# A state-space scan kernel: units of 4 states by 32 channels by 1024 tokens, scanned in place in PSUM

## Chip, cores and metric

The kernel runs on one core of one Trainium2 chip. The metric is the device time of one execution in microseconds (us). Engines are called as in the profile: PE is TensorE (PEld its weight loads), DVE VectorE, ACT ScalarE, POOL GpSimd, SP SyncE, which issues the transfers here. L388 is line 388 of the kernel whose profile is shown. SBUF and PSUM are the two on-chip memories in which the kernel's tiles lie; its matmuls write PSUM tiles.

## The reference, cut to what matters

Three Mambas (selective state spaces) carry the cost. Per Mamba there are 4 images of 4096 tokens, 384 inner channels (`d`) and 16 states (`n`):

```python
xc, z = split(x @ in_w.T)                 # 384 + 384
xc = silu(causal depthwise conv(xc) + conv_b)
dt, B, C = split(xc @ x_w.T)              # 12, 16, 16
dt = softplus(dt @ dt_w.T + dt_b)
def step(h, inp):                         # one token; h is [b, 384, 16]
    dA = exp(dt_t[..., None] * A)
    h = dA * h + (dt_t * x_t)[..., None] * B_t[:, None, :]
    return h, einsum('bdn,bn->bd', h, C_t)
y = (ys + D * xc) * silu(z)
out = y @ out_w.T
```

Stage one runs two Mambas on the same normed input and adds both. Stage two runs a third one with a layer norm before it and a depthwise 3x3 convolution, a second norm and an MLP after it. Stage three (a dynamic convolution and window mixing) is left alone by the change.

## The kernel before

512 tokens of one Mamba are called a stretch: 64 in stage one, 32 in stage two. Channels lie on the partitions, tokens along the free axis. For each of 16 states and 3 chunks of 128 channels there is one chain over a 128x512 piece, and one call of `background.step()`, which traces a piece of the work of the next stretch (projections, convolution, norms) between the scans:

```python
for n in range(n0, n0 + NG):
    for d in range(ND):
        dA = self.psum_a.tile([128, T], F32, name="dA")
        nc.scalar.activation(dA, dt[:, d, :], AF.Exp, scale=self.A[:, d, n : n + 1])
        dBx = self.work.tile([128, T], F32, name="dBx", bufs=2)
        nc.vector.tensor_tensor(dBx, dtx[:, d, :], Bs[:, n - n0, :], ALU.mult)
        h = self.work.tile([128, T], F32, name="h", bufs=3)
        st = self.state[:, d, n : n + 1]
        nc.vector.tensor_tensor_scan(h, dA, dBx, st, ALU.mult, ALU.add)
        nc.vector.tensor_copy(st, h[:, T - 1 : T])
        g = self.work.tile([128, T], F32, name="g", bufs=3)
        nc.gpsimd.tensor_tensor(g, h, Cs[:, n - n0, :], ALU.mult)
        nc.tensor.matmul(ys[d], self.ident, g, start=(n == 0), stop=(n == NS - 1))
        background.step()
# ... softplus: Abs, Exp, Ln on ScalarE, three GpSimd and one VectorE operation
```

The instructions are put into each engine's queue at build time by a scheduler that goes by its own estimate of readiness. On the chip each queue runs in the order so built.

Of the kernel before, what the change touches and what calls it, by code (L numbers as in the profile page):

```python
# [13 lines left out]
F32 = mybir.dt.float32  # L14
AF = mybir.ActivationFunctionType
ALU = mybir.AluOpType
# [4 lines left out]
NB = 4            # batch  # L21
C = 192           # channels
CP = 96           # channels per partition chunk; channel = chunk * 96 + partition
HW = 64           # image side
L = HW * HW       # tokens of one image
DI = 384          # inner width of a mamba
ND = DI // 128    # its chunks of 128
NS = 16           # states
RK = 12           # rank of dt
HID = 768         # hidden width of an MLP  # L30
NH = HID // 128
T = 512           # tokens handled at a time
NT = L // T
NG = 2            # states whose B and C are loaded together
EPS = 1e-5
WIN = 4           # window side
NPOS = WIN * WIN  # positions in a window
NWIN = L // NPOS  # windows of one image


class Pack:
    """Small arrays side by side in one [partitions, columns] array: one load, many views."""
# [27 lines left out]
def chunked(a, p):  # L70
    """[k * p + i, ...] -> [i, k, ...]"""
    a = a.reshape((a.shape[0] // p, p) + a.shape[1:])
    return np.moveaxis(a, 0, 1)


def sedenion_signs():
    """sign[i][k] of e_i * e_(i^k) in the sedenions, whose product is that sign times e_k."""
# [21 lines left out]
class Background:  # L99
    """Work of other stages, traced piece by piece between the steps of the scan in front."""  # L100
# [20 lines left out]
class Norm:  # L121
    """Layer norm of [96, 2, T] over the channels, which lie on the partitions."""
# [52 lines left out]
class Mlp:  # L175
    """gelu(x w1 + b1) w2 + b2 of [96, 2, T]; `last(k, psum)` takes the product before b2."""
# [30 lines left out]
class Mamba:  # L207
    """One selective state space, T tokens at a time: d on the partitions, time along the free
    axis. What it hands from one stretch of tokens to the next stays on chip."""

    def __init__(self, nc, name, taps, ins, const, work, psum, psum_y, psum_a, dram, ident):
        self.nc, self.name, self.taps = nc, name, taps
        self.work, self.psum, self.psum_y, self.psum_a = work, psum, psum_y, psum_a
        self.dram, self.ident = dram, ident
# [8 lines left out]
        self.conv_b, self.dt_b, self.D = w["conv_b"], w["dt_b"], w["D"]  # L223
        self.x_w, self.out_w = w["x_w"], w["out_w"]
        self.A = const.tile([128, ND, NS], F32, name=f"{name}_A")
        nc.scalar.activation(self.A, w["A_log"], AF.Exp)
        nc.vector.tensor_scalar_mul(self.A, self.A, -1.0)
        self.conv = const.tile([128, ND, taps, 128], F32, name=f"{name}_conv")
        for d in range(ND):
            for j in range(taps):  # L230
                nc.vector.tensor_scalar_mul(
                    self.conv[:, d, j, :], ident, w["conv_w"][:, d, j : j + 1]
                )
        self.halo = const.tile([128, ND, taps - 1], F32, name=f"{name}_halo")
        self.state = const.tile([128, ND, NS], F32, name=f"{name}_state")

    def front(self, xn, first, u):
        """All that the scan of these tokens needs; into the dict `u`."""
        nc, K = self.nc, self.taps
        raw = self.work.tile([128, ND, K - 1 + T], F32, name="raw", bufs=1)  # L240
        if first:
            nc.gpsimd.memset(self.halo, 0.0)
        nc.gpsimd.tensor_copy(raw[:, :, 0 : K - 1], self.halo)
        z = u["z"] = self.work.tile([128, ND, T], F32, name="z", bufs=2)
        for e in range(2 * ND):
            ps = self.psum.tile([128, T], F32, name="ps_in", tag="mm")
            for k in range(2):
                nc.tensor.matmul(  # L248
                    ps, self.in_w[:, k, bass.ts(e, 128)], xn[:, k, :], start=(k == 0), stop=(k == 1)
                )  # L250
            nc.scalar.copy(raw[:, e, K - 1 :] if e < ND else z[:, e - ND, :], ps)  # L251
            yield
        nc.gpsimd.tensor_copy(self.halo, raw[:, :, T:])
        xc = u["xc"] = self.work.tile([128, ND, T], F32, name="xc", bufs=2)
        for d in range(ND):
            ps = self.psum.tile([128, T], F32, name="ps_conv", tag="mm")
            for j in range(K):
                nc.tensor.matmul(  # L258
                    ps, self.conv[:, d, j, :], raw[:, d, j : j + T], start=(j == 0), stop=(j == K - 1)
                )  # L260
            nc.scalar.activation(xc[:, d, :], ps, AF.Identity, bias=self.conv_b[:, d : d + 1])
            yield
        nc.scalar.activation(xc, xc, AF.Silu)
        nc.scalar.activation(z, z, AF.Silu)
        yield
# [3 lines left out]
        dbl = self.work.tile([RK + 2 * NS, T], F32, name="dbl", bufs=2)  # L269
        nc.scalar.copy(dbl, ps)  # L270
        bc = u["bc"] = self.dram.tile([2 * NS, T], F32, name="bc", bufs=3)
        nc.sync.dma_start(bc, dbl[RK:, :])
        yield
        dt = u["dt"] = self.work.tile([128, ND, T], F32, name="dt", bufs=2)
        for d in range(ND):
            ps = self.psum.tile([128, T], F32, name="ps_dt", tag="mm")
            nc.tensor.matmul(ps, self.dt_w[:, bass.ts(d, 128)], dbl[:RK, :], start=True, stop=True)  # L277
            nc.scalar.activation(dt[:, d, :], ps, AF.Identity, bias=self.dt_b[:, d : d + 1])
        yield
        # softplus(s) = max(s, 0) + log1p(e), e = exp(-|s|); what 1 + e rounds off is added back  # L280
        e = self.work.tile([128, ND, T], F32, name="sp_e", bufs=1)
        nc.scalar.activation(e, dt, AF.Abs)
        nc.scalar.activation(e, e, AF.Exp, scale=-1.0)  # L283
        dtx = u["dtx"] = self.work.tile([128, ND, T], F32, name="dtx", bufs=2)
        nc.gpsimd.tensor_scalar(dtx, e, 1.0, 1.0, ALU.add, ALU.subtract)  # L285
        nc.gpsimd.tensor_tensor(dtx, e, dtx, ALU.subtract)
        nc.scalar.activation(e, e, AF.Ln, bias=1.0)
        yield
        nc.vector.scalar_tensor_tensor(dt, dt, 0.0, e, ALU.max, ALU.add)
        nc.gpsimd.tensor_tensor(dt, dt, dtx, ALU.add)  # L290
        nc.gpsimd.tensor_tensor(dtx, dt, xc, ALU.mult)  # L291
        yield

    def scan(self, u, first, background):
        nc = self.nc
        if first:
            nc.vector.memset(self.state, 0.0)
        dt, dtx, bc = u["dt"], u["dtx"], u["bc"]
        ys = [self.psum_y.tile([128, T], F32, name=f"y{d}") for d in range(ND)]
        for n0 in range(0, NS, NG):  # L300
            Bs = self.work.tile([128, NG, T], F32, name="Bs", bufs=2)
            Cs = self.work.tile([128, NG, T], F32, name="Cs", bufs=2)
            for t, r in ((Bs, n0), (Cs, NS + n0)):
                nc.sync.dma_start(t, bc[r : r + NG, :].unsqueeze(0).broadcast_to([128, NG, T]))
            for n in range(n0, n0 + NG):
                for d in range(ND):
                    dA = self.psum_a.tile([128, T], F32, name="dA")
                    nc.scalar.activation(dA, dt[:, d, :], AF.Exp, scale=self.A[:, d, n : n + 1])  # L308
                    dBx = self.work.tile([128, T], F32, name="dBx", bufs=2)
                    nc.vector.tensor_tensor(dBx, dtx[:, d, :], Bs[:, n - n0, :], ALU.mult)  # L310
                    h = self.work.tile([128, T], F32, name="h", bufs=3)
                    st = self.state[:, d, n : n + 1]
# [575 lines left out]
```

## Time and profile before

The time is 17661 us (median of 4 runs, 17657 to 17670). Profile lines are in the prediction below; the stages read:

| stage | length, us | DVE busy | PE busy | ACT busy | POOL busy |
|---|---|---|---|---|---|
| one (64 stretches) | 8705 | 8204 | 6358 | 3635 | 5976 |
| two (32 stretches) | 5540 | 3787 | 4470 | 2479 | 2964 |
| three | 3404 | 641 | 2996 | 564 | 2 |

### The profile page before, as it was taken

The numbers are of one execution on the slowest core, as the hardware profiler recorded it, in microseconds if no ns is written. First come the engines' busy times: TensorE is split into PE (matmuls) and PEld (weight loads), VectorE is DVE, ScalarE is ACT, GpSimd is POOL, SyncE is SP. The second block draws the span as 40 slices with busy tenths as digits, with TensorE's granted clock in tenths as the row PEclk, the third lists the DMA queues.
The fourth block names the chain that finished last, engine by engine and source line by source line (L and its number), as shares of the span: only waits on it lengthen the run. The fifth ranks groups of instructions, "written<-read, shape, count | busy, mean of one in ns | idle before, by whom it ended". The sixth has DMA issues, their size and how long they took to land. (4 is left out here: it accounts for less than half of the span.)

```text
span 17649.1 us, 110111 instructions
## 1 busy us (share of the span) xinstructions
PE 13823.4 (78%) x33296; PEld 6083.8 (34%) x33296; DVE 12632.4 (72%) x16123; ACT 6678.3 (38%) x8486; POOL 8941.9 (51%) x5458
## 2 busy tenths in 40 slices
PE   7777777777777777777778878888888869797989
PEld 2222222222222222222223333333333336565656
DVE  8999999999999999999787667676676720202020
ACT  4444444444444444444344444444444411111111
POOL 6766766676667667666565555555555500000000
PEclk8888888878878887888788888888888879898989
DMA  1111111111111111111111111111111110000000
GB/s 66 66 66 66 65 67 67 65 65 67 66 66 66 65 68 66 66 66 64 60 60 56 56 52 58 55 53 55 56 54 54 52 25 6 9 6 11 4 4 6
DMA packets 328063, 902.55 MB, mean 51 GB/s; under 512 B 78196, under 2 KB 111256, under 8 KB 327368
## 3 DMA queue, kind: packets, MB, share of 16 engines
q1 hardware_dynamic: 326704, 892.35, 15.1%
q8 instruction: 261, 4.28, 0.1%
q10 hardware_dynamic: 760, 3.16, 0.1%
q14 instruction: 338, 2.77, 0.0%
HBM read 851.35 MB, written 44.04 MB: 51 GB/s over the span
## 5 line engine op out<-in xcount | busy, mean ns | idle before, releaser
L316 POOL TENSOR_TENSOR g<-h,Cs 128x512 f32<-128x512 f32 x4608 | 6766.6, 1486 | 4030.0 <-PE y L317 2158.8
L317 PE MATMUL y<-g,ident 128*128 128x512 f32 x9216 | 5914.9, 758 | 2370.4 <-POOL g L316 2346.1
L313 DVE TENSOR_TENSOR_SCAN h<-dA,m_state,dBx 128x512 f32<-128x512 f32 x4608 | 5728.5, 1267 | 1121.8 <-POOL g L316 787.9
L310 DVE TENSOR_TENSOR dBx<-dtx,Bs 128x512 f32<-128x512 f32 x4608 | 5734.1, 1252 | 61.8 <-POOL dtx L291 61.8
L308 ACT ACTIVATE dA<-dt,m_A 128x512 f32<-128x512 f32 x4608 | 3158.3, 690 | 6314.1 <-DVE h L313 5977.1
L317 PEld LDWEIGHTS y<-g,ident 128*128 128x128 f32 x9216 | 1859.1, 229 | 5863.7 <-POOL g L316 4824.1
L686 DVE TENSOR_TENSOR y<-plus,neg 96x512 f32<-96x512 f32 x64 | 43.9, 686 | 1599.8 <-ACT neg L685 1599.8
L258 PE MATMUL ps_conv<-raw,m_conv 128*128 128x512 f32 x2112 | 984.5, 604 | 86.8 <-ACT z L251 61.2
L675 PE MATMUL plus<-xn,t 96*96 96x256 f32 x4352 | 1014.6, 380 | 0.0
L675 PE MATMUL minus<-xn,t 96*96 96x256 f32 x3840 | 941.4, 398 | 10.8 <-ACT xn L169 10.8
L248 PE MATMUL ps_in<-xT,m_in_w 96*128 96x512 f32 x1536 | 858.4, 673 | 113.9 <-ACT raw L251 108.6
L613 POOL MEMSET img<- 96x132 f32 x4 | 0.8, 204 | 1795.2 <-DVE xw L660 1795.2
L675 PEld LDWEIGHTS plus<-xn,t 96*96 96x96 f32 x4352 | 710.8, 163 | 339.6 <-issue 134.5
L187 PE MATMUL ps_h<-xn,t 96*128 96x512 f32 x1536 | 764.1, 637 | 76.2 <-ACT hid L190 50.2
L675 PEld LDWEIGHTS minus<-xn,t 96*96 96x96 f32 x3840 | 649.3, 171 | 253.6 <-ACT xn L169 26.7
L196 PE MATMUL ps_o<-hid,t 128*96 128x512 f32 x1536 | 681.6, 601 | 29.1 <-ACT hid L192 29.1
L277 PE MATMUL ps_dt<-dbl,m_dt_w 12*128 12x512 f32 x576 | 459.6, 922 | 243.1 <-ACT dbl L270 233.9
L314 DVE COPY m_state<-h 128x1 f32<-128x1 f32 x4608 | 630.2, 137 | 23.6
L258 PEld LDWEIGHTS ps_conv<-raw,m_conv 128*128 128x128 f32 x2112 | 399.3, 192 | 636.2 <-issue 476.3
L285 POOL TENSOR_SCALAR dtx<-sp_e 128x1536 f32<-128x1536 f32 x96 | 540.7, 5632 | 70.9 <-ACT sp_e L283 70.9
L147 PE MATMUL var<-mean_w,ln_sq 96*128 96x1 f32 x2048 | 315.9, 284 | 327.6 <-ACT ln_sq L142 327.6
L525 PE MATMUL ps_dw<-img,dw 96*96 96x512 f32 x1152 | 538.3, 617 | 0.0
(122 smaller groups left out, 11143.7 us busy)
## 6 DMA issues: line engine op xcount, KB each, us to landing
Bs<-bc SPq DMA_DIRECT2D x768, 512.0 KB, 3.6
Cs<-bc SPq DMA_DIRECT2D x768, 512.0 KB, 3.6
x<-x SPq DMA_DIRECT2D x64, 384.0 KB, 3.3
xt<-in_x SPq DMA_DIRECT2D x32, 384.0 KB, 3.4
x<-o SPq DMA_DIRECT2D x32, 384.0 KB, 2.7
img<-x SPq DMA_DIRECT2D x8, 1536.0 KB, 21.2
out<-o SPq DMA_DIRECT2D x32, 384.0 KB, 3.9
bc<-dbl SPq DMA_DIRECT2D x96, 64.0 KB, 1.6
```

What stands on the lines that cost most here:

```text
L187: nc.tensor.matmul(ps, self.w1[:, k, bass.ts(m, 128)], x[:, k, :], start=(k == 0), stop=(k == 1))
L196: nc.tensor.matmul(ps, self.w2[:, m, bass.ts(k, CP)], h[:, m, :], start=(m == 0), stop=(m == NH - 1),)
L248: nc.tensor.matmul(ps, self.in_w[:, k, bass.ts(e, 128)], xn[:, k, :], start=(k == 0), stop=(k == 1))
L258: nc.tensor.matmul(ps, self.conv[:, d, j, :], raw[:, d, j : j + T], start=(j == 0), stop=(j == K - 1))
L285: nc.gpsimd.tensor_scalar(dtx, e, 1.0, 1.0, ALU.add, ALU.subtract)
L308: nc.scalar.activation(dA, dt[:, d, :], AF.Exp, scale=self.A[:, d, n : n + 1])
L310: nc.vector.tensor_tensor(dBx, dtx[:, d, :], Bs[:, n - n0, :], ALU.mult)
L313: nc.vector.tensor_tensor_scan(h, dA, dBx, st, ALU.mult, ALU.add)
L314: nc.vector.tensor_copy(st, h[:, T - 1 : T])
L316: nc.gpsimd.tensor_tensor(g, h, Cs[:, n - n0, :], ALU.mult)
L317: nc.tensor.matmul(ys[d], self.ident, g, start=(n == 0), stop=(n == NS - 1))
L675: nc.tensor.matmul(ps[:, m, :], w["sed"][:, cc, s ^ k, bass.ts(m, CP)], xn[:, cc, bass.ts(s, NWIN)], start=(n == 0 and cc == 0), stop=(n = ...
```

## The change

Its intent: take the `dt*x*B` multiply off VectorE, where it contended with GpSimd, and the state copy too. To let one instruction multiply by B or C for a whole tile, a unit is now 4 states x 32 channels on the 128 partitions by 1024 columns (one Mamba's 1024 tokens in stage one; two groups of channels by 512 tokens in stage two). `dt`, `dt*x`, B and C are stored to DRAM and read back, repeated over the partitions. The scan overwrites the `Exp` result in PSUM. Three of four C multiplies go to VectorE, the fourth stays on GpSimd. The sum over states becomes a matmul with 32 output columns, four of them in the four column groups. Softplus is one function of ScalarE. 24 units make a stretch, 2304 the whole program. Cut to its core:

```diff
-        nc.scalar.activation(dA, dt[:, d, :], AF.Exp, scale=self.A[:, d, n : n + 1])
-        nc.vector.tensor_tensor(dBx, dtx[:, d, :], Bs[:, n - n0, :], ALU.mult)
-        nc.vector.tensor_tensor_scan(h, dA, dBx, st, ALU.mult, ALU.add)
-        nc.vector.tensor_copy(st, h[:, T - 1 : T])
-        nc.gpsimd.tensor_tensor(g, h, Cs[:, n - n0, :], ALU.mult)
-        nc.tensor.matmul(ys[d], self.ident, g, start=(n == 0), stop=(n == NS - 1))
+    def inputs(self, u):                         # w: S + 3 buffers, 7 in stage one, 5 in two
+        self.nc.gpsimd.tensor_tensor(w, blk["used"]["dtx", c, s], b, ALU.mult)
+    def decay(self, u):                          # a: PSUM, 2 buffers of 2 banks
+        self.nc.scalar.activation(a[:, p, :], ..., AF.Exp, scale=blk["m"].A[:, q, j : j + 1])
+    def run(self, u, on_pool):
+        h = w if on_pool else a
+        nc.vector.tensor_tensor_scan(h[:, p, :], a[:, p, :], w[:, p, :], ..., ALU.mult, ALU.add)
+        nc.scalar.copy(state, h[:, :, self.ts - 1])
+        (nc.gpsimd if on_pool else nc.vector).tensor_tensor(w, h, cc, ALU.mult)
+    def add_up(self, u):                         # once per four units (two in stage two)
+        nc.tensor.matmul(y[32 * g : 32 * g + 32, f : f + T], self.sel, ws[s][:, p, f : f + T], ...)
+    # stream(), at step i:
+            self.load(unit(i + self.AHEAD)); self.inputs(unit(i + 2)); self.decay(unit(i + 1))
+            self.run(unit(i), i % 4 == 1)
+            step(units[i][0])                    # background work, as before
+            self.add_up(unit(i - 1))             # when unit i - 1 ends its group
+            self.gate(unit(i - 3))
+    # evacuations of matmul results: the next matmul is traced first, then a yield
-            nc.scalar.activation(dt[:, d, :], ps, AF.Identity, bias=self.dt_b[:, d : d + 1])
-        ... Abs, Exp, Ln, and four more operations
+            nc.scalar.activation(dt[:, d, :], ps, AF.Softplus, bias=self.dt_b[:, d : d + 1])
```

## The prediction

> **What bounds the kernel now.** I read the page first, then the windows view cut where the work changes, then the groups by form, then single lines. The program is three stages in a row: two Mambas over 512 tokens at a time (64 stretches), a third Mamba with depthwise conv and MLP (32 stretches), and a last stage that the change leaves alone. I cut at the last output store of stage one (8706 us) and the first image load of stage three (14244 us). Columns: length, then busy us (and instructions) of PE, PEld, DVE, ACT, POOL, then clock, DMA share, GB/s.
> ```profile
> 0.00:8705.00 8705.00, 6357.87 (x11773) 2369.33 (x11774) 8203.83 (x10050) 3635.42 (x4761) 5975.76 (x3598) 0.81 0.19 66
> 8705.00:14245.00 5540.00, 4470.03 (x9669) 1766.10 (x9667) 3787.32 (x5097) 2478.89 (x3072) 2963.76 (x1851) 0.85 0.16 54
> 14245.00:17649.00 3404.00, 2995.52 (x11856) 1948.39 (x11856) 641.23 (x976) 563.99 (x653) 2.43 (x10) 0.90 0.05 9
> ```
> Stage one is bound by VectorE: 8204 of 8705 us, 94%, so 136 us per stretch. Stage two is bound by no single engine (PE 81%, DVE 68%) at 173 us per stretch; it waits in chains. Stage three is PE at 88%.
>
> What fills VectorE, from the groups by form:
> ```profile
> L316 POOL TENSOR_TENSOR g<-h,Cs 128x512 f32<-128x512 f32 x4608 | 6766.6, 1486 | 4030.0 <-PE y L317 2158.8 <-DVE h L313 1595.1 <-issue 133.6
> L317 PE MATMUL y<-g,ident 128*128 128x512 f32 x9216 | 5914.9, 758 | 2370.4 <-POOL g L316 2346.1
> L310 DVE TENSOR_TENSOR dBx<-dtx,Bs 128x512 f32<-128x512 f32 x4608 | 5734.1, 1252 | 61.8 <-POOL dtx L291 61.8
> L313 DVE TENSOR_TENSOR_SCAN h<-dA,m_state,dBx 128x512 f32<-128x512 f32 x4608 | 5728.5, 1267 | 1121.8 <-POOL g L316 787.9 <-ACT xc L263 329.2 <-issue 0.6
> L308 ACT ACTIVATE dA<-dt,m_A 128x512 f32<-128x512 f32 x4608 | 3158.3, 690 | 6314.1 <-DVE h L313 5977.1 <-POOL dt L290 235.1 <-DVE m_state L314 90.8
> ```
> A multiply (L310) costs as much as a scan, with equal element counts. The one-line views (min/median/max) show that this is not its own work:
> ```profile
> L310 DVE TENSOR_TENSOR dBx<-dtx,Bs x4608: 656/816/3921, 86.5 to 14091.4; 128x512 f32<-128x512 f32 x192
> L313 DVE TENSOR_TENSOR_SCAN h<-dA,m_state,dBx x4608: 1245/1271/1285, 87.7 to 14094.2; 128x512 f32<-128x512 f32 x192
> L316 POOL TENSOR_TENSOR g<-h,Cs x4608: 1251/1271/2883, 89.0 to 14095.6; 128x512 f32<-128x512 f32 x192
> ```
> The scan never varies; the multiply and its POOL partner do. Alone, L310 takes 0.66 us, so of its 5734 us some 2700 us are spent blocked.
>
> **What the Trainium skill says.** (1) "SBUF — State Buffer", Who interferes with whom: a VectorE instruction with two SBUF inputs contends with a GpSimd instruction that reads SBUF, one with a single SBUF input does not. The trace agrees: L310 (two SBUF inputs) is 0.66 to 3.9 us, L313 (one PSUM, one SBUF) stays within 1.245 to 1.285. (2) "GPSIMD Engine Reference", 3.1: 4497 ns for a 2048-element fp32 tensor_tensor. The trace has 1251 ns at 512 and 3414 at 1536 (L286), 2.11 ns an element, which extends to 4496. (3) "TensorE: Matmul & The Clock Gate", Part 3: matmuls with 32 output columns in distinct column groups run concurrently (2.38 times for three); no 32-column matmul is in this trace.
>
> **The change part by part.** A unit is 4 states x 32 channels x 1024 columns, twice a 128x512 piece: 2304 units in place of 4608 pieces; 24 units per stretch.
>
> *VectorE.* Removed: 4608 dBx multiplies (5734 us, now on POOL), 4608 state copies of 137 ns (630 us, now on ACT). Kept: all scan elements. Added: three quarters of the h*C multiplies (1728 of 1024), a quarter stays on POOL. Scan cost: additions from PSUM take 680 ns at 512 (L508) and 1216 at 1024 (L140), so 1.05 ns per element; L323, which like the scan has a scalar per partition and a PSUM input, takes 737 at 512, so about 200 ns are fixed. If the scan's fixed part is the same, 1271 is 200 plus 2.09 ns per element, and 1024 as one instruction cost 2.34 us, 2.29 back to back (two L313 in a row show 2.44 us, so 50 ns overlap). In stage two it stays two of 512: 2.44. The C multiply reads h from PSUM: L140 is the same form (PSUM and SBUF, 1024 columns), 1.216 us, 1.17 overlapped. Both now have one SBUF input, so POOL should not block them. Four units, stage one: 4x2.29 + 3x1.17 = 12.7 us; stage two: 4x2.44 + 3x1.17 = 13.3 us. Per stretch (six fours): 76 and 80 us. Beside that, stage one has 1.5 gates of 1.22 and 2.5 us of norm and output (L364, L365, L371, L413): floor 80 us. Stage two has two norms (4x1.21), gates, image and MLP additions (7x0.7): floor 90 us.
>
> *POOL.* 1.25 multiplies of 1024 per unit at 178 + 1024x2.11 = 2.34 us: 70 us per stretch, plus 4 for dt*x and 2 for the norm: 76. The Softplus function removes L285, L286, L290 (5.6+3.4+3.7 us) and, with the gate moved to VectorE, L326 (3.9).
>
> *ACT.* Exp at 1024: 692 + 512x0.836 (slope from L142 and L263) = 1.12 us; 24 of them 27 us; state copies 24x0.25 (about L366's fixed cost) = 6; projections, Silu, Softplus 11. Table loads of 1283 ns: the instruction order of the built kernel has 584 in stage one and 480 in stage two (before 439 and 377), so 12 and 19 us per stretch. Total 57 and, with MLP and norms, 85 us.
>
> *PE.* Eight back-to-back instructions of 512 columns took 3.70 us (L258), (3.70-0.59)/7 = 0.44 each, two per fp32 matmul: 0.89 us. The 48 sums per stretch remain 48 matmuls. One behind the other: 43 us, as before. Each matmul is two passes on one column group, so I expect the second pass of one group to run beside the first of the next: half, 21 us. The rest of stage two is 81 matmuls of 512 columns plus small ones, 77 us, plus 3 for D: 101 us halved, 123 if nothing overlaps. Stage one: 56 or 78, no bound.
>
> *DMA.* Each unit brings 0.5 MB (dt, dtx, B, C shares), plus stores: about 33 MB per 1024 tokens of one Mamba, near 185 GB/s at the new pace. Before, 892 MB took 15.1% of the span, so the engines move about 335 GB/s when busy. It fits.
>
> *The wait I expect instead.* dA has two PSUM buffers, and the scan now overwrites it, so a buffer comes free only after the C multiply. In the built order, 227 of 384 fours of stage one place the multiply of unit 0 after the scan of unit 1; then Exp of unit 2 starts only when VectorE has nothing else left: 1.12 + handoff, 1.3 us. That is 0.59x1.3x6 = 4.6 us per stretch. ACT's table switches between two Exps (load, Silu, load: 4 us) I put at 5 us, waits at block starts for the trip through DRAM at 2. Stage one: 80+4.6+5+2 = 92 us, x64 = 5.89 ms. Stage two: PE 101, VectorE 90, ACT 85 in order and coupled; I choose 118 us, x32 = 3.78 ms. Stage three 3.40, start 0.09. Sum 13.16 ms.
>
> **The rivals.** *PE becomes stage two's bound* (no overlap of column groups): 123 us is a floor, about 135 with waits, 4.3 ms, total 13.7. For it: every fp32 matmul in the trace is two instructions (L317 has 9216 for 4608), and both passes of one sum use the same group. *ACT stalls VectorE in both stages*: more loads and only two dA buffers; if each of some 4.5 switches per stretch costs a full 3 us, stage one goes to 100 us, total 13.7. *DMA latency binds*: one SP queue carries stores and loads in order, and loads of a block follow its stores. Against it: loads run six units (20 us) ahead and land in 3.6 us. It would add 5 to 10 us a stretch, 13.8. *PSUM in-place scan is slower*: 10% more per scan is 5.5 us a stretch, 0.5 ms. *All hides well*: 86 and 102 us, 12.25 ms.
>
> **Range and chances.** The low end is the last rival, 12.3; the high end takes two of the bad ones together, 14.3. Even both stages 25% over my figures give 15.6 ms, still 12% faster, so the direction is nearly safe; what is left is an unforeseen serial trip through DRAM.
>
> **What would show it.** L310's successor on POOL near 2.34 us and the C multiply on VectorE near 1.22 with min and median together: contention gone. Scan at 2.34 us: in place in PSUM costs nothing. VectorE 85 to 90% busy in stage one, its idle time ended by the Exp on ACT. PE's sums in stage two: busy time halved or not. Stage lengths 5.9, 3.8, 3.4 ms. I am wrong if the scan is much slower in PSUM, if POOL's multiply is well above 2.4 us, or if VectorE waits on POOL or DMA for most of its idle time.

## More of the kernel before

In stage one the length minus VectorE's busy time is only 501 us: VectorE is the bound. In stage two no engine fills the time.

## The result

The time after is 14731 us (median of 4 runs, 14730 to 14734) against 17661. The ratio is 0.834, with a 95% interval of 0.8328 to 0.8351. A ratio is the mean time of one kernel's fast runs over that of the other's of the same rounds, so not quite the ratio of the medians quoted. The result is correct. So the direction was right, but the time is 1571 us over the prediction and 431 us over the upper end of its range.

The windows view of the kernel after, cut at the same three places (columns as in the prediction):

```profile
0.00:6830.00 6830.00, 4624.21 (x12160) 1449.60 (x12160) 5185.57 (x3365) 3334.64 (x4707) 4819.34 (x2312) 0.78 0.49 167
6830.00:11323.00 4493.00, 3705.09 (x9856) 1384.17 (x9856) 2842.03 (x2563) 2546.56 (x3854) 2433.56 (x1200) 0.82 0.41 130
11323.00:14728.00 3405.00, 2993.60 (x11856) 1946.24 (x11856) 641.37 (x978) 563.93 (x653) 3.35 (x14) 0.90 0.05 9
```

Stage three is untouched (3405 against 3404). Stage one is 6830 us where I had 5.98 ms with the start; stage two 4493 where I had 3.78. VectorE's busy time is what I said: 5186 us in stage one, 81 per stretch (predicted 80), 2842 in stage two, 89 per stretch (predicted 90). So nothing is wrong with the work. What is wrong is the time in which VectorE stands: 6830 - 5186 = 1644 us in stage one (predicted 12 per stretch, 0.77 ms, and 0.09 of start) and 4493 - 2842 = 1651 us in stage two (predicted 118 - 90 = 28 per stretch, 0.90 ms). **The miss is VectorE's idle time, about 0.78 ms more in stage one and 0.75 in stage two.**

The groups by form of the kernel after, for the parts that the prediction timed (busy us, mean ns, then idle time of the engine ahead of them and who ended it):

```profile
L398 DVE TENSOR_TENSOR w<-dA,u_C 128x1024 f32<-128x1024 f32 x1728 | 2060.1, 1210 | 456.2 <-ACT m_state L396 455.7 <-PE ps_y L420 0.5
L388 DVE TENSOR_TENSOR_SCAN dA<-dA,m_state,w 128x1024 f32<-128x1024 f32 x864 | 2006.8, 2346 | 634.0 <-ACT m_state L396 416.3 <-POOL w L369 145.0 <-ACT dA L376 52.4
...
L398 POOL TENSOR_TENSOR w<-w,u_C 128x1024 f32<-128x1024 f32 x576 | 1352.0, 2347 | 622.6 <-ACT m_state L396 622.6
...
L420 PE MATMUL ps_y<-w,sel 128*32 128x512 f32 x9216 | 2616.8, 757 | 1954.1 <-POOL w L398 1303.9 <-DVE w L398 647.3
```

The scan takes 2346 ns (predicted 2.34 us), the C multiply 1210 (1.216), GpSimd's multiply 2347 (2.34), and the 9216 passes of the sums 2617 us in place of 5915 (predicted half). Two idle terms stand out. Ahead of the sums TensorE stood 1954 us, and two thirds of that was ended by GpSimd's C multiply, which does only a quarter of them. And VectorE's waits are ended chiefly by ScalarE's state copy, an instruction of 158 ns. (A wait is put down to what came last: in the timeline below the `Exp` that the scan needs ended only 0.08 us before the copy.)

### How one hold goes round the engines

The timeline of the kernel after, in stage one (start us, duration, engine, instruction; in brackets the engine's idle time ahead of it and who ended it):

```profile
2652.04 9.26 POOL L369 TENSOR_TENSOR w<-u_dtx,u_B 128x1024 f32<-128x1024 f32 x4 [9.58 <-PE ps_y L420]
...
2657.07 4.60 DVE L388 TENSOR_TENSOR_SCAN dA<-dA,m_state,w 128x1024 f32<-128x1024 f32 x2 [4.07 <-ACT m_state L396]
2658.04 0.57 ACT L296 COPY dbl<-ps_x 44x512 f32<-44x512 f32 x1
...
2659.64 1.28 ACT L309 ACT_TABLE_LOAD   x1
2661.26 2.35 POOL L398 TENSOR_TENSOR w<-w,u_C 128x1024 f32<-128x1024 f32 x1
...
2663.66 1.92 PE L420 MATMUL ps_y<-w,sel 128*32 128x512 f32 x2 [6.30 <-POOL w L398]
...
2665.51 3.78 PE L303 MATMUL ps_dt<-dbl,m_dt_w 12*128 12x512 f32 x4
...
2667.62 0.69 ACT L309 ACTIVATE dt<-ps_dt,m_pack 128x512 f32<-128x512 f32 x1 [6.69 <-PE ps_dt L303]
2668.32 1.28 ACT L376 ACT_TABLE_LOAD   x1
...
2669.62 1.12 ACT L376 ACTIVATE dA<-u_dt,m_A 128x1024 f32<-128x1024 f32 x1
2670.67 0.15 ACT L396 COPY m_state<-dA 128x1 f32<-128x1 f32 x1
2670.84 2.36 DVE L388 TENSOR_TENSOR_SCAN dA<-dA,m_state,w 128x1024 f32<-128x1024 f32 x1 [8.05 <-ACT m_state L396]
```

Read it from the top. GpSimd, released by the end of a group of sums, does four B multiplies in a row, and only then, at 2661.26, the C multiply. TensorE's queue has the sums that take that product at its head, so it stands 6.30 us. Behind them wait the matmuls of `ps_dt`, whose input (`dbl`) was ready at 2658.6. They then take 3.78 us for four passes, where the same four take 1.98 at another place of this trace (3003.34): TensorE comes out of the wait at half its rate. ScalarE has the evacuation of `ps_dt` (the instruction that reads the matmul's result out of PSUM) at the head of its queue and stands 6.69 us, with a load of its function table before and one after it. The `Exp` and the state copy, which need nothing of all this, come behind it. VectorE stands 8.05 us. The same sequence, a TensorE wait of 6.3 us ended by GpSimd and a VectorE wait of about 8.0 ended by ScalarE, returns all through stage one: 20 times between 975 and 6526 us.

The Trainium skill states the rule behind it ("PSUM — Partial Sum Buffer", Engine vs sequencer instructions): the queues of ScalarE, VectorE and GpSimd are strict first-in-first-out, and matmuls start and complete in program order. This trace agrees, with 6.30, 6.69 and 8.05 us. On the rate the skill ("TensorE: Matmul & The Clock Gate", Part 1) says that the clock gate passes every pulse or half of them, as the array is found busy or idle; 3.78 against 1.98 us fits.

The waits view, between 600 and 6200 us of the kernel after, for TensorE, ScalarE and VectorE (who waited for whom: us in total, times, longest):

```profile
PE ps_y L420 <- POOL w L398: 878.8, 218, 11.1
PE ps_y L420 <- DVE w L398: 508.9, 172, 11.4
```

```profile
ACT xc L284 <- PE ps_conv L275: 357.4, 74, 10.1
...
ACT dt L309 <- PE ps_dt L303: 175.2, 35, 6.7
```

```profile
DVE dA L388 <- ACT m_state L396: 459.9, 141, 8.1
DVE w L398 <- ACT m_state L396: 216.2, 66, 7.6
...
DVE m_y L433 <- PE ps_y L420: 118.5, 19, 14.0
```

### The profile page after: what moved, and what is told of

Read it like the earlier page. It is cut to its first block, busy times and chain, and to the rows that moved or that the text cites. A ratio compares the mean times of both kernels' runs of the same rounds, so it can differ in the third digit from the quotient of the medians.

```text
span 14728.2 us, 102888 instructions
## 1 busy us (share of the span) xinstructions
PE 11322.9 (77%) x33872; PEld 4780.0 (32%) x33872; DVE 8669.0 (59%) x6906; ACT 6445.1 (44%) x9214; POOL 7256.2 (49%) x3526
## 5 line engine op out<-in xcount | busy, mean ns | idle before, releaser
L369 POOL TENSOR_TENSOR w<-u_dtx,u_B 128x1024 f32<-128x1024 f32 x2304 | 5351.1, 2350 | 2499.2 <-PE ps_y L420 2157.9
L420 PE MATMUL ps_y<-w,sel 128*32 128x512 f32 x9216 | 2616.8, 757 | 1954.1 <-POOL w L398 1303.9
L388 DVE TENSOR_TENSOR_SCAN dA<-dA,m_state,w 128x512 f32<-128x512 f32 (+1 forms) x1872 | 3281.8, 1772 | 970.3 <-ACT m_state L396 570.5
L376 ACT ACTIVATE dA<-u_dt,m_A 128x1024 f32<-128x1024 f32 (+1 forms) x3072 | 2758.3, 902 | 1040.3 <-DVE w L398 818.7
L398 DVE TENSOR_TENSOR w<-dA,u_C 128x1024 f32<-128x1024 f32 x1728 | 2060.1, 1210 | 456.2 <-ACT m_state L396 455.7
L398 POOL TENSOR_TENSOR w<-w,u_C 128x1024 f32<-128x1024 f32 x576 | 1352.0, 2347 | 622.6 <-ACT m_state L396 622.6
L420 PEld LDWEIGHTS ps_y<-w,sel 128*32 128x32 f32 x9216 | 412.9, 121 | 3757.4 <-POOL w L398 1677.0
L388 DVE TENSOR_TENSOR_SCAN w<-dA,m_state,w 128x512 f32<-128x512 f32 (+1 forms) x624 | 1087.1, 1759 | 254.3 <-POOL w L369 156.3
L388 DVE TENSOR_TENSOR_SCAN dA<-dA,w 128x1024 f32<-128x1024 f32 (+1 forms) x432 | 824.7, 1931 | 409.1 <-POOL w L369 160.0
L841 PE MATMUL minus<-xn,t 96*96 96x256 f32 x3840 | 939.2, 397 | 11.8 <-ACT xn L171 11.7
L376 ACT ACT_TABLE_LOAD x527 | 676.1, 1283 | 9.4
L407 PE MATMUL ps_y<-u_xc,m_D 128*128 128x512 f32 x576 | 393.7, 803 | 350.8 <-DVE m_y L433 345.0
```

The lines of the kernel that those rows point to most:

```text
L369: self.nc.gpsimd.tensor_tensor(w, blk["used"]["dtx", c, s], b, ALU.mult)
L376: self.nc.scalar.activation(a[:, p, :], blk["used"]["dt", c, s][:, p, :], AF.Exp, scale=blk["m"].A[:, q, j : j + 1])
L388: nc.vector.tensor_tensor_scan(h[:, p, :], a[:, p, :], w[:, p, :], 0.0 if blk["first"] else state[:, p : p + 1], ALU.mult, ALU.add,)
L398: (nc.gpsimd if on_pool else nc.vector).tensor_tensor(w, h, cc, ALU.mult)
L407: nc.tensor.matmul(y[:, f : f + T], blk["m"].D[:, c, :], blk["used"]["xc", c][:, f : f + T], start=True, stop=False, skip_group_check=True,)
L420: nc.tensor.matmul(y[32 * g : 32 * g + 32, f : f + T], self.sel, ws[s][:, p, f : f + T], start=False, stop=q == NQ - 1, skip_group_check=True,
```

## The experiments

Fifteen kernels ran, all timed in three rounds against the kernel before. "Idle" is the stage's length minus VectorE's busy time, from the windows view. Stage three stayed near 3405 us in all and is left out.

| run | what is different from the kernel after | time, us | ratio to before | stage one: length, idle | stage two: length, idle |
|---|---|---|---|---|---|
| (after) | - | 14731 | 0.834 | 6830, 1644 | 4493, 1651 |
| state_dve | state copy on VectorE | 14555 | 0.8244 | 6599, 1349 | 4544, 1511 |
| no_switch | no table switches (wrong) | 14163 | 0.8022 | 6507, 1365 | 4248, 1404 |
| light_pe | one tap per convolution (wrong) | 14442 | 0.8178 | 6942, 1753 | 4100, 1270 |
| w_more | 9 and 6 `w` buffers | 14531 | 0.8229 | 6770, 1637 | 4368, 1536 |
| four_gone | the four above together (wrong) | 13508 | 0.7649 | 6274, 974 | 3819, 832 |
| grouped | Silu and Softplus in one piece each | 14660 | 0.8302 | 6754, 1556 | 4481, 1631 |
| conv_twice | Mamba convolutions done twice | 15426 | 0.8735 | 7239, 2071 | 4779, 1930 |
| no_pool_c | all C multiplies on VectorE | 14334 | 0.8118 | 6510, 985 | 4411, 1337 |
| pool_first | GpSimd's C multiply on unit 0 of 4 | 14437 | 0.8175 | 6510, 1408 | 4531, 1686 |
| npc_conv_twice | no_pool_c + conv_twice | 14739 | 0.8345 | 6703, 1155 | 4623, 1544 |
| npc_light_pe | no_pool_c + light_pe (wrong) | 14194 | 0.8039 | 6408, 891 | 4360, 1299 |
| npc_grouped | no_pool_c + grouped | 14192 | 0.8035 | 6435, 906 | 4346, 1271 |
| npc_grouped_sd1 | that + state copy of stage one on VectorE | 14095 | 0.7982 | 6342, 714 | 4336, 1261 |
| npcgs_pin | that + norm operations of stage two pinned later | 14090 | 0.7981 | 6335, 708 | 4349, 1269 |
| h_sbuf | h written to SBUF, not over dA | 15196 | 0.8608 | 7158, 1002 | 4636, 1406 |

The letters of theories in the quoted expectations were given anew in each batch, and each text says what they stand for.

### First batch: four suspects, one at a time

The waits named the state copy, the table loads, TensorE's late results and the `w` buffers. Each was taken away alone.

**state_dve**: the copy leaves ScalarE's queue.

```diff
-        nc.scalar.copy(state, h[:, :, self.ts - 1])
+        nc.vector.tensor_copy(state, h[:, :, self.ts - 1])
```

> One edit: the state copy goes from ACT to VectorE. Theory A (VectorE is held by ACT's queue in order: evacuations that wait for TensorE and table switches stand ahead of Exp and of the state copy): the copy leaves that queue, but Exp stays in it, and VectorE gets 2304 copies of 0.14 us, 0.32 ms, so only part of the 1.26 ms of waits for the copy comes back: 14.2 to 14.6 ms. Rival D (the copy itself on the path, between scan and C multiply on another engine, is the cause): all of the 1.26 ms less 0.32 comes back, 13.8 ms. Rival B (too few w buffers, POOL and TensorE wait for each other): 14.7 to 15.0 ms.

Measured 14555 us (14547 to 14567): 176 us less, as theory A had it. Stage one gains 231, stage two loses 51. The loss has a visible part: 192 copies of two columns from SBUF average 781 ns, one of them taking 5.1 us, while the 576 of the same shape from PSUM average 152. The trace of the kernel after shows what the copy's place costs: each of the 1728 C multiplies on VectorE starts 0.03 to 8.3 us after its unit's copy on ScalarE has ended, and none before, though it does not read what the copy writes.

**no_switch**: Silu, Sqrt and Gelu become Identity and Softplus becomes Exp, so that one table serves.

> Wrong result on purpose: Silu, Softplus, Sqrt and Gelu of the two scan stages replaced by Identity and Exp, so that no table is switched there (1064 loads of 1.283 us gone from ACT, all else in place). Theory A: VectorE's waits for ACT hold 193 us of table loads directly and as much again in what the loads delay: 14.1 to 14.4 ms. Rival E (table switches are the main thing that my prediction mis-sized): 13.5 ms. Rivals B and C (w buffers, TensorE load): 14.6 to 14.7.

Measured 14163 us: 568 us less, in theory A's range, for 1141 table loads of 1283 ns (1.46 ms of ScalarE), all but three taken away, 0.50 us a load. (72 of them were in stage three, whose length did not change; for the others it is 0.53.) It is the largest of the four, but about a third of the miss.

**light_pe**: one matmul per convolution (of 4, 3 and 9).

```diff
-            for j in range(K):
+            for j in (K - 1,):                      # start and stop both True
```

> Wrong result on purpose: one tap of each convolution is kept (4 or 3 taps to 1, 9 to 1), which takes 9 matmuls of 0.89 us from each stretch of stage one and 22 from each of stage two: 0.51 and 0.63 ms of TensorE work, none of any other engine. Theory A and C (background results come late from TensorE and are waited for in order by ACT and VectorE): 13.8 to 14.2 ms, and ACT's idle time behind ps_conv falls. If TensorE is only busy and not in the way (B, D, E): 14.6 ms or more.

Measured 14442 us, between the two expectations: 289 us less. Stage two gained 393 us and stage one lost 112 though TensorE did less. Its granted clock there fell from 0.78 to 0.74:

```profile
0.00:6942.00 6942.00, 4281.30 (x11008) 1276.60 (x11008) 5188.92 (x3365) 3344.18 (x4719) 4815.67 (x2312) 0.74 0.48 164
```

ScalarE's waits behind `ps_conv` did fall, as expected (357 to 103 us between 600 and 6200 us). Taking this work away did not shorten stage one. I took that for the clock at this point; see conv_twice and npc_light_pe.

**w_more**: two more `w` buffers in stage one, one more in stage two. There is no room for them, so the second Mamba shares the first one's convolution weights. That is wrong in principle, though its output stayed within the tolerance.

> Wrong result on purpose (stage one's second Mamba uses the first one's conv taps, which frees the memory): 9 in place of 7 buffers for w in stage one, 6 in place of 5 in stage two. Rival B (POOL waits 2.16 ms for TensorE to give w back, TensorE waits for POOL's product, and VectorE waits 0.6 ms for POOL): 14.0 to 14.3 ms, POOL's idle behind ps_y mostly gone. Theory A: POOL's wait shrinks, VectorE's waits for ACT stay, 14.5 to 14.7 ms.

Measured 14531 us, as theory A had it: 200 us less, most of it in stage two.

### Second batch: grouping, loading, removing

**four_gone**: all four edits in one kernel.

> Wrong on purpose: the four edits of the first batch in one kernel (state copy on VectorE, no table switches, one tap per convolution, more w buffers). Alone they gained 176, 568, 289 and 200 us. Additive: 13.50 ms. If they are the same waits seen from several sides: 13.8 to 14.1 ms. If each hides behind the others: 13.2 ms or less, which would account for the whole miss against 13.16.

Measured 13508 us. The single gains add up to 1233 us, the kernel gained 1223, so they are not one wait seen from four sides. By stage the sums agree less well (502 against 556 us in stage one, 712 against 674 in stage two), and npc_light_pe below shows a gain that does not add, so the close total is partly luck. Even without all four, 0.35 ms of the miss is left. Stage two is then 3819 us, 119 per stretch, what I had predicted for the whole; stage one still idles 974 us.

**grouped**: the built ScalarE queue has more loads than the functions need: the scheduler sets an `Exp` between two Softplus evacuations and between the two Silu calls. Here the evacuations add the bias only and one Softplus over 128x1536 follows; `xc` and `z` share a tile for one Silu.

```diff
-        nc.scalar.activation(xc, xc, AF.Silu)
-        nc.scalar.activation(z, z, AF.Silu)
+        nc.scalar.activation(xz, xz, AF.Silu)
-            nc.scalar.activation(dt[:, d, :], ps, AF.Softplus, bias=self.dt_b[:, d : d + 1])
+            nc.scalar.activation(dt[:, d, :], ps, AF.Identity, bias=self.dt_b[:, d : d + 1])
+        nc.scalar.activation(dt, dt, AF.Softplus)
```

> Correct result. The three Softplus evacuations become Identity evacuations and one Softplus over 128x1536, the two Silu calls one over 128x3072, so that no Exp can be built in between; the built ScalarE program has 759 table loads instead of 1141, 382 x 1.283 = 0.49 ms less ScalarE work, against 96 x about 1.5 us more. Theory A (ScalarE's own queue is what VectorE waits for, table loads in it): no_switch took 1141 loads away and gained 568 us, 0.50 us a load, so 382 give about 190 us: 14.50 to 14.60 ms. Rival T (TensorE's lateness sets the pace, the loads fill waits): within 60 us of 14.73. Rival L (one Silu of 2.9 us in a piece holds an Exp back): slower than 14.75.

Measured 14660 us: 71 us less, not 190. The loads did go. Groups of ScalarE between 600 and 6200 us, first of the kernel after, then of grouped (L376 is `Exp`, L309 and L310 are Softplus; each line counts the loads ahead of that function):

```profile
L376 ACT ACT_TABLE_LOAD x242 | 310.5, 1283 | 4.3
L309 ACT ACT_TABLE_LOAD x111 | 142.4, 1283 | 2.1 <-issue 0.2
```

```profile
L376 ACT ACT_TABLE_LOAD x134 | 171.9, 1283 | 2.4
...
L310 ACT ACT_TABLE_LOAD x53 | 68.0, 1283 | 0.9
```

ScalarE had less to do and waited longer for TensorE instead. That is what the rival with TensorE's lateness says.

**conv_twice**: the matmuls of the Mamba convolutions are done twice, the second time over the first. The result is correct.

> Correct result: the matmuls of both Mamba convolutions are done twice, the second time over the first. At the durations of after that is 0.79 ms more TensorE time in stage one and 0.28 in stage two. Theory T (the time a result of TensorE takes is waited for): the longer convolution delays its evacuations, 0.3 to 0.6 ms slower, 15.0 to 15.3 ms, with ScalarE's waits for ps_conv about doubled. Rival K (light_pe gained nothing in stage one because fewer matmuls lower the granted clock): the clock of stage one rises from .78 by .02 or more, the other matmuls get faster, and the time stays within 150 us of 14.73. Rival H (TensorE is hidden as its total fits, as I predicted): within 100 us.

Measured 15426 us: 695 us more, above the 0.3 to 0.6 of theory T. Stage one is 409 us longer for 437 us more TensorE time (5062 against 4624 busy): as much as if almost all of it were waited for. ScalarE's waits for `ps_conv` did not double, as theory T also had it (357 to 281 us between 600 and 6200 us); those for other matmuls grew (`raw` for `ps_in` to 253, `xT` for `ps_t` to 199). Rival H, my own claim that PE is hidden in stage one, is refuted; the rival with the clock is too (0.80 against 0.78, and slower).

**no_pool_c**: GpSimd keeps only the B multiplies. The result is correct.

```diff
-                self.run(unit(i), i % 4 == 1)
+                self.run(unit(i), False)
```

> Correct result: all C multiplies on VectorE, 576 x 1.21 = 0.70 ms more VectorE work, 1.35 ms less GpSimd work. Theory V (VectorE is the floor, its waits are other engines'): 0.6 to 0.75 ms slower, 15.35 to 15.5 ms. Rival G (GpSimd's tardiness in the one unit of four costs what the trace of after lays to it, 104 + 34 us in stage one and 264 in stage two): 15.0 to 15.15 ms.

Measured 14334 us (14325 to 14347), **397 us faster, with 0.70 ms more work for VectorE.** Both expectations had the wrong sign. VectorE's idle time fell by 659 us in stage one and 314 in stage two. Windows of stages one and two:

```profile
0.00:6510.00 6510.00, 4526.25 (x12160) 1444.02 (x12160) 5525.40 (x3749) 3340.06 (x4689) 3937.78 (x1928) 0.80 0.51 175
6510.00:10922.00 4412.00, 3669.19 (x9856) 1313.55 (x9856) 3074.56 (x2755) 2542.13 (x3850) 1990.85 (x1008) 0.84 0.40 133
```

And the waits of ScalarE and of VectorE between 600 and 6200 us, to be held against those of the kernel after:

```profile
ACT xc L284 <- PE ps_conv L275: 52.3, 59, 1.5
```

```profile
DVE dA L388 <- ACT m_state L396: 262.8, 102, 4.4
...
DVE w L398 <- ACT m_state L396: 28.4, 29, 2.2
DVE m_y L433 <- PE ps_y L420: 12.8, 14, 1.5
```

ScalarE's waits for the convolution fell from 357 to 52 us (longest 10.1 to 1.5), VectorE's for the copy ahead of the C multiply from 216 to 28, for the gate (L433) from 119 to 13. TensorE has the same matmuls as before; its results come in time now. My own bookkeeping had put only 138 us of stage one's idle time to GpSimd (104 + 34), because it stopped at the engine that was running last.

The 659 us are not all the hold's. VectorE works 340 us longer in this stage one, and that alone may hide some of the others' lateness: in h_sbuf below, which keeps GpSimd's product, VectorE works longer still and idles as little (1002 us). The stage's length is the safer measure: 320 us less.

### Third batch: is it GpSimd's work, or its place?

**pool_first**: the same work on every engine; GpSimd's C multiply is moved from the second to the first unit of four, which puts it one unit further ahead of the sums that take it.

```diff
-                self.run(unit(i), i % 4 == 1)
+                self.run(unit(i), i % 4 == 0)
```

> Correct result. GpSimd does the C multiply of the first unit of four instead of the second; the amount of work on every engine is unchanged. Theory G (GpSimd's product, which in the trace of after begins a median 4.6 us after its scan has ended, holds the sums, and with them all of TensorE's queue, ScalarE's evacuations and the next scan): the product gets one more unit, 3.5 to 4.3 us, before the sums want it; TensorE's waits for it fall below half of their 1304 us, and the time to 14.1 to 14.45 ms. Rival V (what counted in no_pool_c was GpSimd's 2.35 us of work, a late B product): 14.65 ms or more, TensorE's waits moved only.

Measured 14437 us, at the edge of theory G's range: 294 us less. Stage one is 6510 us, as short as that of no_pool_c. The product begins a median 2.2 us after its scan, not 4.9. TensorE's waits for products, 878.8 us for GpSimd's and 508.9 for VectorE's in the kernel after, are in the same window:

```profile
PE ps_y L420 <- DVE w L398: 770.9, 295, 7.4
PE ps_y L420 <- POOL w L398: 327.1, 112, 6.4
```

So half of what TensorE no longer waits for GpSimd it now waits for VectorE, and still stage one's 320 us hang on when that product comes, with nothing else changed. They do not all come by way of TensorE. VectorE's idle time falls by 236 us; its busy time falls by 83, nearly all of it in one instruction of the norm, whose duration (min/median/max, ns) was in the kernel after and is here:

```profile
L511 DVE TENSOR_SCALAR xs<-xt,mv,rs x128: 366/1701/2527, 21.2 to 6257.2; 128x192 f32<-128x192 f32 x128
```

```profile
L511 DVE TENSOR_SCALAR xs<-xt,mv,rs x128: 364/376/2530, 21.0 to 5947.5; 128x192 f32<-128x192 f32 x128
```

It takes 183 us in all in the kernel after and 97 here. In the trace of the kernel after, all 77 that took over 0.8 us ran beside a GpSimd instruction and ended 0.12 us after its end, and of the other 51, 50 ran while GpSimd stood. So GpSimd blocks it, though it has a single large SBUF input (and two scalars per partition). Stage two does not gain (38 us longer): two units make a group there. Why, no run shows.

**npc_conv_twice**: the doubled convolutions without GpSimd's product.

> Correct result: no_pool_c with the convolutions' matmuls done twice. Theory G (TensorE's background work was waited for because TensorE stood behind GpSimd's product; without that it has slack): 1.06 ms more TensorE work costs less than 350 us over no_pool_c, 14.40 to 14.68 ms. Rival T (TensorE is late by its own work, in either kernel): 600 to 700 us more again, 14.95 ms or more.

Measured 14739 us: 405 us more than no_pool_c, between theory G (under 350) and T (600 or more). In stage one the doubling now costs 193 us in place of 409, in stage two 212 in place of 286. So about half of what TensorE's work costs in stage one goes with GpSimd's product, and half stays; how far it is only that VectorE works longer in no_pool_c, and so may hide more, is not separated.

**npc_grouped**: no_pool_c with grouped.

> Correct result: no_pool_c with Silu and Softplus each in one piece, 382 table loads fewer. grouped alone gained 71 us. If waits for TensorE hid the loads there (theory G), they show now: 0.5 us a load, about 190 us, 14.10 to 14.20 ms. Rival L (the long Silu of about 2.9 us and the later Softplus give back what the loads gained, whatever else): 14.24 ms or more.

Measured 14192 us: the grouping gains 142 us here (71 before), within theory G's range and 0.37 us a load. The table loads were partly hidden behind waits for TensorE.

**npc_grouped_sd1**: the same, and the state copy of stage one on VectorE.

> Correct result: npc_grouped with the state copies of stage one on VectorE (1536 of about 0.1 us), which takes them out of ScalarE's queue between scan and C multiply. In state_dve that gained 233 us in stage one; there part of it was waits that no_pool_c no longer has (VectorE's waits for the copy in stage one: after 860 us, no_pool_c about 300). Theory: 60 to 150 us below npc_grouped, 13.98 to 14.12 ms. Rival: VectorE is now near its floor in stage one and its own 0.15 ms of copies eats the gain: within 50 us of npc_grouped.

Measured 14095 us (14087 to 14104), correct: 97 us less again, as the theory had it. Its ratio to the kernel before is 0.798, so it beats both kernels. Stage one:

```profile
0.00:6342.00 6342.00, 4446.34 (x12160) 1438.95 (x12160) 5627.88 (x5285) 2888.88 (x2905) 3937.08 (x1928) 0.81 0.53 180
```

VectorE is busy 89% of it (76% in the kernel after).

### Fourth batch: what was open

**h_sbuf**: does the scan in place in PSUM give what it should? Here `h` goes to SBUF in all units.

```diff
-        h = w if on_pool else a
+        h = w
```

> Correct result: every scan writes h to the SBUF tile w instead of over dA in PSUM, so the C multiply on VectorE has two SBUF inputs, as the removed dB*x multiply had. Theory S (two SBUF inputs contend with GpSimd, one does not): the C multiply's median goes from 1.21 us to 1.6 or more with a wide spread, GpSimd's B multiply too; 1728 x 0.4 or more = 0.7 ms of VectorE time, less what its 2 x earlier release of the PSUM tile gives back (Exp waits of 290 us in stage one): 15.0 to 15.6 ms. Rival R (the early release of dA is worth more than the contention): under 14.7 ms.

Measured 15196 us: 465 us slower, in theory S's range. Groups by form of VectorE and GpSimd in h_sbuf:

```profile
L398 DVE TENSOR_TENSOR w<-w,u_C 128x1024 f32<-128x1024 f32 x1728 | 3552.5, 2069 | 252.2 <-ACT m_state L396 252.2
```

```profile
L369 POOL TENSOR_TENSOR w<-u_dtx,u_B 128x1024 f32<-128x1024 f32 x2304 | 6019.3, 2637 | 1839.5 <-PE ps_y L420 1776.4 <-issue 43.1 <-DMA u_dtx<-k_dtx 12.1
```

With two SBUF inputs the C multiply takes 2069 ns on average, not 1210, and GpSimd's B multiply 2637, not 2350. The medians, of which theory S spoke, do not show it (1315 ns, under its 1.6 us, and 2347 as before); the cost is in the tail, up to 11.8 us for a C multiply (1.23 in the kernel after). That is 1.48 ms of VectorE. It comes back in part: VectorE idles 642 us less in stage one. How much of that is dA's earlier release (the scans' waits for `Exp` fell from 266 to 90 us in the whole program) and how much only a VectorE that works 970 us longer there, this run does not separate. The contention that the prediction wanted to be rid of is real, and PSUM is what avoids it.

**npc_light_pe**: no_pool_c with one tap per convolution.

> Wrong on purpose: no_pool_c with one tap per convolution. In light_pe stage one got 111 us longer and stage two 389 shorter. Theory G (stage one there waited for GpSimd's product, whatever TensorE did): with that gone the loss is gone, stage one within 60 us of no_pool_c's 6510, and stage two, where TensorE's amount of work counts, again 250 to 400 us shorter than its 4411: 13.90 to 14.15 ms. Rival K (fewer matmuls lower TensorE's granted clock, and its late results cost stage one time in any case): stage one 80 us or more above 6510.

Measured 14194 us, slower than theory G's range. In stage one the loss of light_pe is gone (102 us shorter than no_pool_c, where theory G had 60 at most). The clock hardly fell here (0.79 against 0.80), so this does not clear the clock of light_pe's loss. In stage two I was wrong: only 51 us came of it, not 250 to 400. The granted clock fell there from 0.84 to 0.78, a rival that no run takes apart. VectorE's idle time there ends near 1.3 ms whether the taps go, GpSimd's product goes, or both (1270, 1337, 1299).

**npcgs_pin**: in stage two the two operations of the norm and the image addition on VectorE, which wait for a matmul just issued, are traced two steps later and queued behind a scan (short form of the edit, made at three places):

```diff
+        yield
+        yield
+        with after_scan():                         # queued behind the latest scan
             nc.vector.tensor_tensor(d, d, rb.unsqueeze(1).broadcast_to([CP, 2, T]), ALU.mult)
```

> Correct result: npc_grouped_sd1, and in stage two the norm's two operations and the image addition of VectorE, which wait for a matmul, are traced two steps later and queued behind a scan of that time. Theory O (VectorE stands at the head of its own queue before a matmul that is still running: 318 + 304 us of waits for rb and mean are left in the whole program, of which some 400 us in stage two): 100 to 300 us less, 13.8 to 14.0 ms. Rival W (the built order moves them by a scan or less, or TensorE needs the time anyway): within 60 us of 14.09 ms.

Measured 14090 us, within 5 us of npc_grouped_sd1, as the rival had it. The built order shows why this settles little: the reciprocal ahead of the multiply was put later too, so the multiply still follows it directly and still waits for `rb`.

## Why the prediction was right or wrong

- **What bounds it, and the direction: right.** VectorE's floor of stage one was 80 us per stretch predicted and 81 measured, and its removed multiply was slow by contention, as h_sbuf shows from the other side. "Both now have one SBUF input, so POOL should not block them" holds for the C multiply (1192 to 1226 ns) and the scan; it is no general rule, as L511 in pool_first and the two-column copies in state_dve show.
- **The durations: right, but for TensorE's.** Scan, C multiply and GpSimd's multiply came within 1%. The sums' busy time fell to 0.44 of before, but to 27 us per stretch and not to 21: "43 us, as before" was reckoned from full-rate passes, while the L317 line in the prediction itself gives 5915/96 = 62. The rival "PSUM in-place scan is slower" is out: 2346 ns. "No overlap of column groups" is out: 284 ns per pass in place of 642.
- **DMA latency: hidden, as predicted.** The engines were busy 49% in stage one and no wait for a transfer reaches the first places of VectorE's, ScalarE's or TensorE's waits.
- **The idle terms that I named in stage one: right in size.** When each idle gap of VectorE between 600 and 6830 us (60 stretches) is followed to what the engine that ended it was doing, `Exp` accounts for some 310 us, 5.2 per stretch (predicted 4.6), and table loads, Silu and evacuations on ScalarE for 295 us, 4.9 (predicted 5). For the loads a run agrees: no_switch shortens stage one by 323 us, 5.0 per stretch. For the `Exp` it is an attribution from the trace.
- **The step that failed: "Stage one: 56 or 78, no bound" for PE, and with it "a quarter stays on POOL", booked at its 2.34 us and as time beside other work.** I compared totals of engines and asked where each total fits. I did not ask at whose queue's head each result is wanted. GpSimd's product began a median 4.9 us after its scan (4.6 in my expectation), mostly behind B multiplies (4.5 of a mean 5.4 us in stage one). TensorE's sums stood at the head of its queue for it, the background matmuls behind them, ScalarE's evacuations behind those, and the `Exp` or state copy that VectorE needs behind those. This term was absent from my sum. Measured: pool_first shows, with no work changed, that 320 us of stage one's length, of the 850 that I missed there, hang on the product's place alone (some 85 of them by way of L511); no_pool_c shortens it by the same 320.
- **A second step that failed: the state copies "now on ACT", booked as 6 us of ScalarE's time.** Each stands between its scan and its C multiply, in ScalarE's queue. state_dve puts them back on VectorE and shortens stage one by 231 us, 3.6 per stretch. So the idle time ended by "the Exp on ACT", my sign, came out otherwise: in the whole program the copy ended 1259 us of the waits of scan and C multiply, `Exp` 266. Of the rivals, "ACT stalls VectorE in both stages" came nearest, but not by the cost of switches alone (0.57 ms in no_switch).
- **My sign of being wrong did not fire.** "VectorE waits on POOL or DMA for most of its idle time" was not so (POOL ended 609 us of the scans' waits, of 3295 us idle in the two stages), although a late result of POOL cost 320 us: the last releaser was another engine.
- **My own second guess also failed.** Before no_pool_c I expected it to be slower by at least 0.27 ms. An idle gap counted against the engine that was working last hides the engine that made that one late.
- **Stage two: "coupled; I choose 118 us" was mis-sized, 140 measured.** ScalarE and VectorE are at or under what I had (80 and 89 us per stretch, predicted 85 and 90). PE's term is short: 3705 us, 116 per stretch against 101, at a granted clock of 0.82, where I had taken the durations of a full-rate run. But it is not a floor: light_pe gives 128 per stretch with PE at 100. Removing table loads, taps and waiting for buffers took 7.7, 12.3 and 3.9 us per stretch (the state copy added 1.6), and together 21. That this equals the miss of 22 proves nothing, since loads and taps were part of my 118 too; it shows that several costs, none of them a bound, make up the stage. How they share one wait is **open**: npc_light_pe says that taps and GpSimd's product overlap, and npcgs_pin failed to move the order it was to test.
- **Also open:** why light_pe lost 112 us in stage one. It is gone without GpSimd's product (npc_light_pe); whether the built order or the lower clock (0.74) made it, no run tells.

## What to carry to other kernels

Engines that run in order form one chain: a result that comes late stops not only its consumer but all that is queued behind the consumer, on that engine and on the next. So a sum of busy times that fits does not show that the work is hidden; look, for each handoff between two engines, what stands behind the waiting instruction in its queue, and give the slowest engine's results the longest lead or take that engine off the path, even at the price of more work on the busiest engine (no_pool_c: 0.70 ms more work, 0.40 ms less time). And when an idle gap is traced back, follow it past the engine that worked last to the one that made it late, and confirm by a run that moves work without changing it.

## What the Trainium skill lacked or had wrong

- "ScalarE: Activation LUTs", What ACT_TABLE_LOAD costs, gives 1283 ns and a drain of about 1380 more. The load agrees (1283 in every group). No such drain shows: a load at 2668.32 us follows an evacuation that ended at 2668.31, and `Exp` starts at 2669.62, 0.02 after its end. In the kernel after, 1137 of the 1141 loads start within 0.1 us of the end of ScalarE's instruction before, and 988 are followed within 0.1 us by the next. In the whole program a load cost 0.50 us of time (no_switch) and 0.19 to 0.37 (grouped, npc_grouped).
- No page gives a time in ns for tensor_tensor_scan (one gives a rate relative to other instructions). These runs: 1280 ns for 128x512 and 2346 for 128x1024 in place in PSUM (2.08 ns per element), 1265 and 2335 with the result in SBUF.
- "TensorE: Matmul & The Clock Gate", Part 3, has a measured column packing for three tiles (2.38 times) but not for four of 32 columns in fp32. Here a pass fell from 642 to 284 ns on average, 2.26 times, in a queue shared with other matmuls.
- "SBUF — State Buffer", Who interferes with whom, gives the rule and single ratios, but not the average price in a mixed stream. h_sbuf: a VectorE multiply with two SBUF inputs 2069 ns in place of 1210, GpSimd's beside it 2637 in place of 2350. A two-column copy from SBUF averaged 781 ns, from PSUM 152 (state_dve; the 92 of 192 that took over 0.4 us each ended 0.03 us after a GpSimd instruction beside them), and L511 with one large SBUF input had a median of 1701 ns in one order of the same work and 376 in another (pool_first).
- "PSUM — Partial Sum Buffer", Engine vs sequencer instructions, states that queues run in order, but no page says what that costs across three engines: here 6.30 us on TensorE became 6.69 on ScalarE and 8.05 on VectorE.
